# Attention output projection: two token tiles multiplied during the last attention units, and its input requested one group earlier

## The chip, the cores and the metric

The kernel runs on one core of a Trainium2 chip. The metric is the device time of one execution in microseconds (us). Engines are named as the profile names them: PE (TensorE, matrix products; PEld its weight loads), DVE (VectorE), ACT (ScalarE), POOL (GpSimd), SP (SyncE; SPq is its queue, from which this kernel issues all its DMAs).

## What is computed

For each of two images of 48 x 48 = 2304 tokens with 768 channels, in float32, one attention layer and one spectral layer, each added to its input:

```
q, k, v = split(groupnorm(x) @ qkv_w + qkv_b)              # 12 heads of 64
attn = softmax(q * 64**-0.5 @ k.T + rel_h + rel_w)         # rel_h, rel_w: products of q with tables
x = x + (attn @ v) @ proj_w + proj_b
f = rfft2(groupnorm(x))                                    # over the 48 x 48 grid
o1 = gelu(block_matmul(f, w1) + b1)                        # 8 blocks of 96 channels, complex
o2 = softshrink(block_matmul(o1, w2) + b2, 0.01)
x = x + irfft2(o2)
```

The change touches the line with proj_w, and the end of the attention ahead of it.

## The kernel before

The kernel is written in a tile framework. It derives the semaphores, and it chooses each engine's order of instructions when it builds the program: by program position among the instructions that it reckons ready. Instructions that go through the wrapper InOrder (L58) keep their program order on their engine; all of these carry L66 in the profile. The others can move.

The two images are handled one after the other (block_kernel, L1006), each in three stages.

*Attention* (L139). The unit of work is a pair of heads with 128 queries; there are 108 units (L451), numbered n. In the loop (L471) step n computes the scores of unit n (PE into PSUM banks, DVE adds the position term that POOL wrote into s, L320), the exponentials (ACT), and 32x32 transposes on DVE. exchange (L379) spreads them over the partitions into a buffer pT, of which there are two: per half unit six DMAs on SP and two ACT copies. weigh (L393) multiplies pT by the values two steps later: at step n it takes unit n-2. finish copies the result, and for every third unit writes it to the DRAM tensor oT; the inverses of the softmax denominators go to inv_d through a transpose ps_i. At the steps from 102 to 108 the loop calls late() (L533), which runs the next of seven steps of a Projection (L549): weights in two halves, nothing, tokens(0), nothing, the bias, and values_bias (L581). values_bias multiplies the value bias through the projection (L591), for the first image only. Its seventh call, at step 108, comes after weigh of unit 106 and ahead of weigh of unit 107 in the program.

tokens(g) (L602) fetches the attention output of 384 tokens (three token tiles of 128): one DMA from oT (L610), two from inv_d (L612), then one POOL multiply of the two (L616). There are two buffers for the product, taken in turn, and one for the inverses.

*Projection* (project_out, L620). x2 is six parts of x, each of four rows of 96 tokens. Each part is loaded (L632) and gets the projection bias on POOL, row by row (L634, four instructions a part). After part 0 come constants and tokens(1). Then the loop over 18 token tiles (L661): every third tile calls tokens for its group, if it isn't there yet, and takes it. For each half of the 768 output channels, six products (L670) go into one PSUM bank, and DVE adds the bank onto the rows of x2 (L679). Each float32 product is two matmul records in the profile, so a tile has 24. Between the tiles stand over_w (L642: eight matmul records ps_y, four ACT copies and a DMA to y_d, L658) and tile_stats (L700) for the finished rows: DVE sums (L703) and scales them (L704), POOL subtracts the mean (L706), ACT squares, DVE sums again (L710).

*Spectral* (L742) follows.

PSUM has seven banks in one pool, ps_b, for scores, projections, products and transforms, and one bank for ps_o. The projection's weights, bias, products and inverses lie in one SBUF area (tag span) that held the normalized x in attention before. The parts x2 take SBUF that attention's pools give back at its end.

```python
            if len(order) - 6 <= n <= len(order):
                late()
...
        if t % 3 == 0:
            if t // 3 not in pr.o:
                pr.tokens(t // 3)
            o_sb = pr.o[t // 3]
```

Of the kernel before, what the change touches and what calls it, by code (L numbers as in the profile page):

```python
# [9 lines left out]
F32 = mybir.dt.float32  # L10
# [6 lines left out]
P = 128  # L17
# [6 lines left out]
NCC = C // P  # L24
NT = S // P
# [7 lines left out]
UQ = 384  # L33
# [24 lines left out]
class InOrder:  # L58


    def __init__(self, tc, engine):
        self.tc, self.engine = tc, engine
# [474 lines left out]
def shifts(t):  # L537


    size = {0: P, 32: 32, 64: 64, 96: 32}  # L540
    p = 0
    while p < P:
        hp, q = divmod(t * P + p, 2 * HW)
        n = min(P - p, 2 * HW - q, size[p], size[q])
        yield p, hp, q, n
        p += n


class Projection:  # L549


    def __init__(self, tc, k, a, oT, inv_d, span, ps_b, dram):
        self.nc = nc = tc.nc
        self.k, self.a, self.ps_b, self.dram = k, a, ps_b, dram
        self.oT_v = oT.rearrange("(cc p) s -> p cc s", p=P)
        self.inv_d = inv_d
        self.whole = span.tile([P, NCC * S], F32, tag="span", name="proj")
        self.w = self.whole[:, : NCC * C].rearrange("p (cc f) -> p cc f", f=C)
        self.pb = self.whole[:, NCC * C : (NCC + 1) * C]
        self.o = {}  # L560
        w_v = a["proj_w"].rearrange("(cc p) f -> p cc f", p=P)
        half = NCC // 2
        self.steps = [
            lambda: nc.sync.dma_start(out=self.w[:, :half], in_=w_v[:, :half]),
            lambda: nc.sync.dma_start(out=self.w[:, half:], in_=w_v[:, half:]),
            lambda: None,
            lambda: self.tokens(0),
            lambda: None,
            self.bias,
            self.values_bias,  # L570
        ]

    def step(self):
        self.steps.pop(0)()
# [6 lines left out]
    def values_bias(self):  # L581


        nc, k = self.nc, self.k
        if k.pb_d is not None:
            return
        for hf in range(2):
            cols = slice(hf * UQ, (hf + 1) * UQ)
            ps = self.ps_b.tile([P, 512], F32, tag="b", name="ps_pb")
            for cc in range(NCC):  # L590
                nc.tensor.matmul(  # L591
                    ps[:, :UQ],
                    lhsT=k.bv[:, cc : cc + 1].to_broadcast([P, P]),
                    rhs=self.w[:, cc, cols],
                    start=(cc == 0),
                    stop=(cc == NCC - 1),
                )
            nc.vector.tensor_tensor(self.pb[:, cols], ps[:, :UQ], self.pb[:, cols], ALU.add)
        k.pb_d = self.dram.tile([C], F32, tag="pb_d", name="pb_d")
        nc.sync.dma_start(out=k.pb_d, in_=self.pb[0, :])  # L600

    def tokens(self, g):  # L602

        nc = self.nc
        at = [(NCC + 1) * C + i * NCC * UQ for i in range(3)]
        o_sb, inv = (
            self.whole[:, c0 : c0 + NCC * UQ].rearrange("p (cc s) -> p cc s", s=UQ)
            for c0 in (at[g % 2], at[2])
        )
        nc.sync.dma_start(out=o_sb, in_=self.oT_v[:, :, g * UQ : (g + 1) * UQ])  # L610
        for h in range(2):
            nc.sync.dma_start(  # L612
                out=inv[h * HD : (h + 1) * HD],
                in_=self.inv_d[:, g // 3, h, g % 3, :].partition_broadcast(HD),
            )
        nc.gpsimd.tensor_tensor(o_sb, o_sb, inv, ALU.mult)  # L616
        self.o[g] = o_sb


def project_out(tc, k, x_b, pr, pools, y_d, x2, stats, constants):  # L620

    nc = tc.nc
    ps_b, small, work = pools
    bank = lambda name: ps_b.tile([P, 512], F32, tag="b", name=name)
    R = 2 * HW
    x_v = x_b.rearrange("(t p) c -> p t c", p=R)  # L630
    for i, part in enumerate(x2):
        nc.sync.dma_start(out=part, in_=x_v[:, i * XP : (i + 1) * XP, :])  # L632
        for j in range(XP):
            nc.gpsimd.tensor_tensor(part[:, j, :], part[:, j, :], pr.pb[:R], ALU.add)  # L634
        if i == 0:
            constants()
            pr.tokens(1)
    row = lambda hp: x2[hp // XP][:, hp % XP, :]
    local = small.tile([R, HW // 2, NG], F32, tag="local", name="local")
    dev = small.tile([R, HW // 2, NG], F32, tag="dev", name="dev")  # L640

    def over_w(g):  # L642

        y1 = work.tile([YP, 2, C], F32, tag="y1", name="y1")
        part = x2[2 * g // XP]
        t0 = 2 * g % XP
        for s in range(C // SC):
            ch = slice(s * SC, (s + 1) * SC)
            ps = bank("ps_y")
            nc.tensor.matmul(  # L650
                ps[:YP, : 2 * SC],
                lhsT=k.fw,
                rhs=part[:, t0 : t0 + 2, ch],
                start=True,
                stop=True,
            )
            nc.scalar.copy(y1[:, :, ch], ps[:YP, : 2 * SC].rearrange("p (t c) -> p t c", c=SC))
        nc.sync.dma_start(out=y_d[:, 2 * g : 2 * g + 2, :], in_=y1)  # L658

    done = turned = 0  # L660
    for t in range(NT):  # L661
        if t % 3 == 0:
            if t // 3 not in pr.o:
                pr.tokens(t // 3)
            o_sb = pr.o[t // 3]
        for hf in range(2):
            cols = slice(hf * UQ, (hf + 1) * UQ)
            acc = bank("acc")
            for cc in range(NCC):
                nc.tensor.matmul(  # L670
                    acc[:, :UQ],
                    lhsT=o_sb[:, cc, (t % 3) * P : (t % 3 + 1) * P],
                    rhs=pr.w[:, cc, cols],
                    start=(cc == 0),
                    stop=(cc == NCC - 1),
                )
            for p, hp, q, n in shifts(t):
                dst = row(hp)[q : q + n, cols]
                nc.vector.tensor_tensor(dst, acc[p : p + n, :UQ], dst, ALU.add)  # L679
        while (turned + 1) * 2 * R <= (t - 1) * P:  # L680
            over_w(turned)
            turned += 1
        while (done + 1) * R <= (t + 1) * P:
            tile_stats(
                nc,
                lambda name: work.tile([R, C], F32, tag="st", name=name),
                row(done),
                local[:, done, :],
                dev[:, done, :],
            )  # L690
            done += 1
    while turned < HW // 4:
        over_w(turned)
        turned += 1
    mean, rstd = join_stats(nc, k, small, bank, local, dev)
    nc.vector.tensor_copy(stats[:, 0, :], mean)
    nc.vector.tensor_copy(stats[:, 1, :], rstd)


def tile_stats(nc, work, xt, local, dev):  # L700

    x3 = xt.rearrange("p (g d) -> p g d", d=GC)
    nc.vector.tensor_reduce(local, x3, AX.X, ALU.add)  # L703
    nc.vector.tensor_scalar(local, local, 1.0 / GC, None, ALU.mult)  # L704
    xc = work("st_xc").rearrange("p (g d) -> p g d", d=GC)
    nc.gpsimd.tensor_tensor(  # L706
        xc, x3, local[:, :, None].to_broadcast([xt.shape[0], NG, GC]), ALU.subtract
    )
    nc.scalar.activation(xc, xc, AF.Square)  # L709
    nc.vector.tensor_reduce(dev, xc, AX.X, ALU.add)  # L710
# [31 lines left out]
class Spectral:  # L742
# [50 lines left out]
    def bank(self, name):  # L793
        return self.ps_b.tile([P, 512], F32, tag="b", name=name)
# [363 lines left out]
```

## Time and profile before

| what | value |
|---|---|
| median of 3 runs | 3907.91 us (3903.24 to 3908.79) |
| the profiled execution | 3910.83 us |
| its span, first to last instruction | 3908.90 us |
| mean granted clock of PE | 0.967 |
| PE busy | 3660.4 us, 94% |
| DVE busy | 2987.5 us, 76% |
| ACT busy | 2528.1 us, 65% |
| POOL busy | 2117.0 us, 54% |
| products L670 | 864 records, 291.6 us busy, PE idle 24.5 us before them |
| POOL multiply L616 | 12 instructions, 5065 ns each |

The profile is one execution. Its times count from the span's start. A line of the view in order of time gives the start, the length, the engine, the line and the operation, what is written and read, the shape and how many instructions were merged; in brackets stands how long the engine was idle before and which work ended that. The chain of waits lists the start, the length and the piece of work. The first image's projection lies at about 1504 to 1694 us, the second's at about 3457 to 3647 us.

### The profile page before, as it was taken

What the parts mean: (1) busy time and instruction counts of PE and PEld (TensorE: products, weight loads), DVE (VectorE), ACT (ScalarE), POOL (GpSimd) and SP (SyncE); (2) the same over time, 40 slices, a digit from 0 to 9 for tenths busy, and PEclk for the clock granted to TensorE, in tenths of its full rate; (3) what the DMA queues carried; (4) which work ended last, traced back from release to release, by engine and by line L of the source; (5) the groups of instructions that cost most, each with busy time, mean ns of one, the idle gap of its engine ahead of it and who ended that gap; (6) DMA issues with size and microseconds to landing.
All of it is one profiled execution on the core that took longest, in us unless ns stands there. A gap on an engine that the chain in (4) does not pass through costs nothing.

```text
span 3908.9 us, 83210 instructions
## 1 busy us (share of the span) xinstructions
PE 3660.4 (94%) x31416; PEld 2591.6 (66%) x31416; DVE 2987.5 (76%) x6642; ACT 2528.1 (65%) x3585; POOL 2117.0 (54%) x682
## 2 busy tenths in 40 slices
PE   6999999999999888989959999999999999779898
PEld 4677776767777655566536777767677776545665
DVE  5688888888889885654546888888888888856544
ACT  3588888888888882222135888888888888722221
POOL 2566666666666666422225666666666666664221
PEclk7999999999999998999989999999999999989999
DMA  2477777777777888534424777777777778884344
GB/s 93 100 169 172 171 175 165 170 172 174 173 167 166 175 197 197 130 84 122 139 85 104 176 171 170 168 174 168 172 172 167 176 164 177 189 197 127 85 121 131
DMA packets 496094, 606.22 MB, mean 155 GB/s; under 512 B 180109, under 2 KB 311053, under 8 KB 495694
## 3 DMA queue, kind: packets, MB, share of 16 engines
q1 hardware_dynamic: 495694, 600.89, 66.1%
q8 instruction: 250, 4.10, 0.5%
q14 instruction: 150, 1.23, 0.1%
HBM read 130.81 MB, written 87.67 MB: 56 GB/s over the span
## 4 chain that ended last, share of the span: by engine, by line
PE 80%; DVE 6%; DMA 6%; POOL 4%; SPq 3%; issue 1%; ACT 1%; POOLq 0%; DVEq 0%; ACTq 0%
PE ps_o L66 20%; PE ps_s L66 19%; PE ps_proj L66 14%; PE ps_v L66 8%; PE acc L670 5%; DVE s L66 4%; PE ps L905 4%; POOL s L320 2%; SPq L66 2%; DMA pT<-s 2%; PE ps_z L853 2%; PE ps L878 2%; PE ps L882 2%; PE ps_u L936 2%; PE ps_r L66 1%
## 5 line engine op out<-in xcount | busy, mean ns | idle before, releaser
L320 POOL TENSOR_TENSOR s<-rhw 128x2304 f32<-128x2304 f32 x432 | 1744.8, 4060 | 1096.4 <-DMA pT<-s 575.9
L66 DVE CUSTOM_DVE_ANT_0 s<-ps_s,s 128x512 f32<-128x512 f32 (+1 forms) x2160 | 1223.3, 633 | 401.0 <-issue 225.6
L66 ACT ACTIVATE s<-s,nm 128x1152 f32<-128x1152 f32 x864 | 1074.7, 1245 | 445.9 <-DVE nm L66 415.1
L66 DVE STREAM_TRANSPOSE s<-s 128x1152 f32<-128x1152 f32 x864 | 1111.8, 1344 | 5.5 <-ACT s L66 5.5
L66 ACT COPY pT<-s 32x1152 f32<-32x1152 f32 x864 | 993.2, 1149 | 28.8 <-PE ps_o L66 13.3
L66 PE MATMUL ps_o<-pT,v 128*64 128x128 f32 x15552 | 924.5, 279 | 77.7 <-DMA pT<-s 41.7
L66 PEld LDWEIGHTS ps_o<-pT,v 128*64 128x64 f32 x15552 | 872.7, 140 | 140.6 <-issue 79.0
L66 PE MATMUL ps_s<-kT,qT 64*128 64x512 f32 (+1 forms) x4320 | 922.4, 559 | 23.2 <-DVE mx L66 19.3
L66 PEld LDWEIGHTS ps_s<-kT,qT 64*128 64x128 f32 x4320 | 432.5, 187 | 462.6 <-issue 335.6
L66 PE MATMUL ps_proj<-xnT,w 128*128 128x384 f32 (+1 forms) x2016 | 597.4, 450 | 11.8 <-issue 11.8
L66 PEld LDWEIGHTS ps_proj<-xnT,w 128*128 128x128 f32 x2016 | 360.5, 191 | 219.2 <-DVE mx L66 41.1
L670 PE MATMUL acc<-proj 128*128 128x384 f32 x864 | 291.6, 497 | 24.5 <-POOL proj L616 12.4
L66 PEld LDWEIGHTS ps_v<-w,xnT 128*128 128x128 f32 x2592 | 297.6, 194 | 21.8 <-DVE mx L66 21.8
L66 PE MATMUL ps_v<-w,xnT 128*128 128x128 f32 x2592 | 309.8, 279 | 0.0
L922 POOL TENSOR_TENSOR spectrum<-spectrum 128x480 f32<-128x480 f32 x80 | 96.2, 1203 | 326.7 <-DVE spectrum L921 323.9
L670 PEld LDWEIGHTS acc<-proj 128*128 128x128 f32 x864 | 168.0, 195 | 144.6 <-issue 21.3
L709 ACT ACTIVATE st_xc<-st_xc 96x768 f32<-96x768 f32 (+1 forms) x84 | 71.1, 847 | 266.7 <-POOL st_xc L706 266.7
L679 DVE TENSOR_TENSOR x<-acc,x 32x384 f32<-32x384 f32 (+2 forms) x216 | 119.5, 553 | 80.2 <-PE acc L670 76.3
L66 DVE DVE_READ_ACCUMULATOR2_ANT mx<- 128x1 f32 x2160 | 180.1, 83 | 0.0
L66 ACT ACTIVATION_READ_ACCUMULATOR s<-s,nm 128x1 f32 x864 | 161.2, 187 | 0.0
L710 DVE TENSOR_REDUCE dev<-st_xc 96x32 f32<-96x768 f32 (+1 forms) x84 | 78.9, 948 | 96.4 <-ACT st_xc L709 96.4
L706 POOL TENSOR_TENSOR st_xc<-x,local 96x768 f32<-96x768 f32 x48 | 70.9, 1481 | 148.2 <-DVE local L704 128.8
(87 smaller groups left out, 2275.1 us busy)
## 6 DMA issues: line engine op xcount, KB each, us to landing
pT<-s SPq DMA_DIRECT2D x2592, 144.0 KB
t<-rel SPq DMA_DIRECT2D x144, 189.0 KB
rhw<-t SPq DMA_DIRECT2D x144, 144.0 KB
y_d<-y SPq DMA_DIRECT2D x24, 672.0 KB
y<-y_d SPq DMA_DIRECT2D x40, 360.0 KB
u_d<-spectrum SPq DMA_DIRECT2D x40, 360.0 KB
u<-u_d SPq DMA_DIRECT2D x48, 300.0 KB
xt<-in_x SPq DMA_DIRECT2D x12, 1152.0 KB
```

What stands on the lines that cost most here:

```text
L66: return lambda *args, **kw: self.tc.keep_in_program_order(op(*args, **kw))
L320: nc.gpsimd.tensor_tensor(s[:, h, :].rearrange("p (y x) -> p y x", x=HW), rhw[:, x, h, :HW][:, :, None].to_broadcast([P, HW, HW]), rhw[:, ...
L670: nc.tensor.matmul(acc[:, :UQ], lhsT=o_sb[:, cc, (t % 3) * P : (t % 3 + 1) * P], rhs=pr.w[:, cc, cols], start=(cc == 0), stop=(cc == NCC - 1),
L679: nc.vector.tensor_tensor(dst, acc[p : p + n, :UQ], dst, ALU.add)
L709: nc.scalar.activation(xc, xc, AF.Square)
L710: nc.vector.tensor_reduce(dev, xc, AX.X, ALU.add)
L853: nc.tensor.matmul(ps[:BS, w * 96 : (w + 1) * 96], lhsT=self.y2[s, j][:, w, i * BS : (i + 1) * BS], rhs=k.fh, start=True, stop=True,)
L878: nc.tensor.matmul(ps[:BS, :400], lhsT=w1[:, wa, i, :], rhs=zf[:, 0, fs], start=True, stop=False,)
L882: nc.tensor.matmul(ps[:BS, :400], lhsT=w1[:, wb, i, :], rhs=zf[:, 1, fs], start=False, stop=True,)
L905: nc.tensor.matmul(ps[64 * r : 64 * r + 64, w * BS : (w + 1) * BS], lhsT=self.o1[:, ri, f0 : f0 + 64], rhs=w2[:, (0, 2, 1, 0)[2 * r + ri], ...
L922: nc.gpsimd.tensor_tensor(val, val, clip, ALU.subtract)
L936: nc.tensor.matmul(ps[: 2 * HW, :480], lhsT=k.ih, rhs=d2[:, c0 : c0 + 480], start=True, stop=True)
```

## The change

The seventh late step, still at step 108, is a new method last: values_bias as before, then the products of token tiles 0 and 1, in both halves, into four banks of ps_b that are kept in a dictionary accs. The projection loop takes these banks instead of computing them; DVE's adds stay where they were. Secondly, the loop asks for a group of tokens three tiles before it is used: at tile 3 for tiles 6 to 8, at tile 6 for tiles 9 to 11, and so on. Groups 0 and 1 are asked for where they were. The number of instructions doesn't change.

```diff
-            self.values_bias,
+            self.last,
         ]
+        self.accs = {}
...
+    def last(self):
+
+        self.values_bias()
+        for t in range(2):
+            for hf in range(2):
+                self.product(t, hf)
+
+    def product(self, t, hf):
+
+        o_sb = self.o[t // 3]
+        acc = self.ps_b.tile([P, 512], F32, tag="b", name="acc")
+        for cc in range(NCC):
+            self.nc.tensor.matmul(
+                acc[:, :UQ],
+                lhsT=o_sb[:, cc, (t % 3) * P : (t % 3 + 1) * P],
+                rhs=self.w[:, cc, hf * UQ : (hf + 1) * UQ],
+                start=(cc == 0),
+                stop=(cc == NCC - 1),
+            )
+        self.accs[t, hf] = acc
+
...
     for t in range(NT):
-        if t % 3 == 0:
-            if t // 3 not in pr.o:
-                pr.tokens(t // 3)
-            o_sb = pr.o[t // 3]
+        if t % 3 == 0 and 0 < t < NT - 3:
+            pr.tokens(t // 3 + 1)
         for hf in range(2):
             cols = slice(hf * UQ, (hf + 1) * UQ)
-            acc = bank("acc")
-            for cc in range(NCC):
-                nc.tensor.matmul(
-                    acc[:, :UQ],
-                    lhsT=o_sb[:, cc, (t % 3) * P : (t % 3 + 1) * P],
-                    rhs=pr.w[:, cc, cols],
-                    start=(cc == 0),
-                    stop=(cc == NCC - 1),
-                )
+            if (t, hf) not in pr.accs:
+                pr.product(t, hf)
+            acc = pr.accs.pop((t, hf))
```

## The prediction

> **What bounds the kernel now.** First the whole. TensorE (PE) is busy 94% of the span, but an early product helps only if PE is what comes last where its time is freed. Granted clock of the run: 0.967. So I read PE's instructions in order of time around the end of attention, then the same stretch on GpSimd (POOL) and on SyncE's queue (SPq). First batch, PE: unit 107's scores, then the attention weighting of units 105, 106 and 107 (ps_o), then the projection (L670).
>
> ```profile
> 1464.24 5.34 PE L66 MATMUL ps_s<-kT,qT 64*128 64x512 f32 x20
> 1469.51 8.01 PE L591 MATMUL ps_pb<-proj,bv 128*128 128x384 f32 x24
> 1478.88 4.15 PE L66 MATMUL ps_o<-pT,v 128*64 128x128 f32 x72 [1.37 <-DMA pT<-s]
> 1487.12 6.87 PE L66 MATMUL ps_o<-pT,v 128*64 128x128 f32 x72 [4.08 <-DMA pT<-s]
> 1497.13 6.98 PE L66 MATMUL ps_o<-pT,v 128*64 128x128 f32 x72 [3.14 <-DMA pT<-s]
> ...
> 1504.15 31.13 PE L670 MATMUL acc<-proj 128*128 128x384 f32 x96
> ...
> 1560.74 5.92 PE L670 MATMUL acc<-proj 128*128 128x384 f32 x12 [8.69 <-DVE x L679]
> 1572.63 7.78 PE L670 MATMUL acc<-proj 128*128 128x384 f32 x15 [5.96 <-POOL proj L616]
> ```
>
> The reader is to see two things. The weighting waits each time for the exchange (pT<-s), so there are holes of some 8.6 us that products could fill. And the projection is stopped later, before token tile 6: the 5.96 us wait ends with POOL's multiply of attention output by inverse denominators (L616) for tiles 6 to 8. From 1573 to 1694 the table of stretches shows PE busy 121.00 of 121 us. So the stage ends when tile 6 starts, plus a fixed PE-bound rest. **The start of tile 6 is the gate**; PE time saved before it is only waited away. So what does POOL do before it?
>
> ```profile
> 1516.03 5.06 POOL L616 TENSOR_TENSOR proj<-proj 128x2304 f32<-128x2304 f32 x1
> 1522.75 1.48 POOL L706 TENSOR_TENSOR st_xc<-x,local 96x768 f32<-96x768 f32 x1 [1.66 <-DVE local L704]
> 1524.20 14.17 POOL L634 TENSOR_TENSOR x<-x,proj 96x768 f32<-96x768 f32 x8
> 1538.33 2.92 POOL L706 TENSOR_TENSOR st_xc<-x,local 96x768 f32<-96x768 f32 x2
> 1541.21 14.15 POOL L634 TENSOR_TENSOR x<-x,proj 96x768 f32<-96x768 f32 x8
> 1555.54 1.48 POOL L706 TENSOR_TENSOR st_xc<-x,local 96x768 f32<-96x768 f32 x1 [0.18 <-DVE local L704]
> ...
> 1567.53 5.04 POOL L616 TENSOR_TENSOR proj<-proj 128x2304 f32<-128x2304 f32 x1 [1.79 <-DMA proj<-inv_d]
> ```
>
> POOL is full from 1522.75 to 1565.7: twenty bias adds on x (L634, 1.77 us each) and the statistics' subtractions (L706). Only then comes the gate's multiply, and it idles a mere 1.79 us for its data. SPq shows why the data is late:
>
> ```profile
> 1508.74 7.63 SPq L632 DMA_DIRECT2D x<-in_x  x5
> 1543.64 0.33 SPq L658 DMA_DIRECT2D y_d<-y  x1
> 1544.08 0.40 SPq L610 DMA_DIRECT2D proj<-oT  x1
> 1544.58 1.79 SPq L612 DMA_DIRECT2D proj<-inv_d  x1
> ...
> 1559.78 0.58 SPq L612 DMA_DIRECT2D proj<-inv_d  x1
> ```
>
> The request for tiles 6 to 8 stands behind a store (L658), its last half 15 us later. The second batch repeats it, 1953.15 us later: tile 6 starts at 3525.89. Its chain of waits has one more link that matters:
>
> ```profile
> 3431.82 5.64 PE ps_o L66 x72
> 3437.52 0.59 SPq L66
> ...
> 3445.24 5.41 DMA pT<-s
> 3450.96 6.30 PE ps_o L66 x72
> ```
>
> Weighting 105 releases the pT buffer into which unit 107 is exchanged: from its end to weighting 107 there are 13.5 us of DMA issue and landing (in the first batch from SPq's 1484.36 to 1497.13, 12.8 us). Work put ahead of weighting 105 therefore delays the end of attention one for one.
>
> [...] the 96x32 tensor_scalar of L704 needs 0.18 us when POOL is idle and 10.22 us at 1545.17, until the block of eight L634 ends. [...] the same 72 matmuls take 4.15 us behind work and 6.87 us after 4.08 us of idleness. [...] between 1510 and 1540 the DMA share is 1.00 to 1.07 at 223 to 233 GB/s[...].
>
> **The change, part by part.** I write d for the delay of attention's end.
>
> *Four products moved ahead.* A tile is 24 matmul records, 7.74 us in the chain (x24), so 0.3225 us each. Two tiles are 48 records, 15.5 us. They issue no DMA; they hold four of the seven PSUM banks, beside two of the bias product and one for the transpose ps_i, which fits. Their input is ready when L616 has run for tiles 0 to 2: 1476.27+5.10 = 1481.4 (second batch 3427.57+5.10 = 3432.7). Weightings 105 to 107 keep their order; products stand before weighting 107 in the program, so all are issued before it. What is unknown is how many, k, are issued before weighting 105, whose operands come at 1478.9 and 3431.8, about when the products' do. I take k near 0: weighting 105 is earlier in the program and its data come no later. The other end, k = 48, is a rival below.
>
> With k = 0, first batch: 1483.0 (end of 105) + 15.5 + 4.15 (106, warm) = 1502.7, weighting 107 ends at 1506.8 instead of 1504.1: d = 2.7. Second batch: 3437.4+15.5+4.15 = 3457.1, end 3461.2 instead of 3457.25: d = 4.0. Behind that end wait SPq's stores of oT and inv_d, the inverse loads for tiles 3 to 5 and x parts 1 to 5; all come d later. In exchange PE enters the stage with two tiles done, 15.5-d ahead, and has tiles 2 to 5 done around 1506.8+31+5.2 = 1543. This lead buys nothing at the gate.
>
> *What it buys on VectorE and POOL.* The adds of tile 0 no longer wait for PE (1508.28 now); they start with the first biased x rows, about 1503.5. The statistics of rows 0 and 1 come about as much sooner. POOL's idle time in front of the x block (5.70+1.66 us) then shrinks until the next limit: the inverse for tiles 3 to 5 lands at 1515+d, its multiply ends at 1520+d, and the twenty bias adds start there, not at 1524.2. First batch: 1522.7, a gain of 1.5. Second batch: L616 started at 3469.43 on its data, so 3469.43+5.06+4.0 = 3478.5, against 3477.34: a loss of 1.2.
>
> *Request three tiles ahead.* Nothing is added: three DMAs (L610, L612 twice) and one multiply a group, moved from tile 6 to tile 3, and so on. On SPq they go behind the five x parts and ahead of the y_d store, waiting there only for tile 2's products and the L616 before; behind them wait the y_d stores, which PE then doesn't need soon. Their 2.36 MB at 228 GB/s take 10.4 us after the x parts (landed at 1540.2): 1551+d, against 1567.4. So the 1.79 us (second batch 1.89) of waiting on POOL go. But the multiply stays behind the bias adds, which are earlier in the program and whose data land earlier; what is late next is POOL itself. With the same four subtractions (rows 2 to 5) before it as now, the gate moves by 1.5+1.8 = 3.3 us and by -1.2+1.9 = 0.7 us, 4.0 together. If rows 6 and 7 also get ahead of it, 1.48 x 2 = 3.0 a batch are lost; if rows 4 and 5 fall behind it, 3.0 a batch are won. PE stands idle longer before tile 6: the first 24 records take 10.3 to 10.7 us there now; a colder start (ps_z at 3658.46: 8.29 for 50 records instead of 4.25) may cost up to 1 more a batch; I take 0.5.
>
> Later groups: tile 9's multiply ended at 1586.4 while PE needed it about 1601, so asking earlier gains nothing. Hidden by POOL's 43 us block: all of the product lead. If that cover went, up to 15.5-d a batch would show.
>
> **Sum.** 4.0-1.0 = 3.0 us off the profiled execution's 3910.83 (span 3908.90 and 1.93 around it). That execution is 2.9 over the median 3907.91. Against the median: **3905**.
>
> **Rivals.** *The queues come out better (B).* If the multiply for tiles 6 to 8 goes right behind the last bias add, it ends at 1522.7+35.4+5.05 = 1563.2 (gain 9.4) and 3478.5+40.5 = 3519.0 (gain 6.9): 16 together, **3892**; ahead of the last four adds another 7.1 a batch, 3878. For it: its data are there by 1554, and VectorE's statistics may be too late for POOL. Against: the bias adds come first in the program, and subtractions fit while x is loading.
>
> *Slower (C): products ahead of weighting 105.* The bias product of the first batch (L591) already stands there, pulled ahead of weightings 105 and 106, which speaks for it; the late L616 speaks against. With k = 48 weighting 105 starts at 1481.4+15.5 = 1496.9, ends at 1501.0, and 12.8 us later weighting 107 starts at 1513.8 instead of 1497.13: d = 16.7. Second batch 3432.7+15.5+4.15+13.5 = 3465.9 instead of 3450.96: d = 15. The x parts go with it: 4.2-16.7+1.8 = -10.7 and 2.8-15+1.9 = -10.3, **3929**. It decides from the point where 107's exchange ends later than PE: 1481.4+0.3225k+4.15+12.8 over 1505.1, k over 21; at k = 34 it is about half.
>
> *The products aren't moved in effect:* if PE's order leaves them behind weighting 107, d = 0 and only the earlier request counts, some 4 us: inside the forecast's case.
>
> **Chances.** Forecast, 3900 to 3911: 0.41. B, 3878 to 3899: 0.36. C, over 3916: 0.23. A measurement of this kernel can tell about 0.2%, 7.8 us, from no change, so the forecast counts as the same, B as faster, C as slower. Range 3885 to 3925: it leaves out the upper half of C and the best end of B.
>
> **What would show it.** PE: four acc products between weightings 105 and 107, no holes there, 107 ending 3 to 4 us later; then 15 us or more of idleness before tile 6, ended by L616. POOL: no wait for inv_d before that multiply, the bias adds still ahead of it. SPq: L610 right behind the x parts. I am wrong if the multiply for tiles 6 to 8 stands before the last bias adds, if weighting 105 comes after the products, or if VectorE, not POOL, ends the wait before tile 6.

## The result and the profile after

| | before | after |
|---|---|---|
| median of 6 runs | 3906.57 us (3903.24 to 3908.79) | 3924.93 us (3921.81 to 3926.38) |
| the profiled execution, its span | 3910.83 us, 3908.90 us | 3924.16 us, 3922.40 us |
| mean granted clock of PE | 0.967 | 0.966 |
| PE idle before the products | 24.5 us | 64.9 us |
| busy time of the products | 291.6 us | 298.9 us |

The ratio is 1.0047, with a 95% interval of 1.0034 to 1.0060: the change costs 18.4 us. That is near rival C's 3929, not the forecast's 3905. The two profiled executions stand 13.3 us apart.

First PE in order of time, from unit 107's scores on, as in the prediction, first image. L615 is the line of the products now.

```profile
1469.81 8.01 PE L592 MATMUL ps_pb<-proj,bv 128*128 128x384 f32 x24
1481.33 10.99 PE L615 MATMUL acc<-proj 128*128 128x384 f32 x28 [3.51 <-POOL proj L638]
1492.25 4.15 PE L66 MATMUL ps_o<-pT,v 128*64 128x128 f32 x72
1496.33 6.72 PE L615 MATMUL acc<-proj 128*128 128x384 f32 x20
1502.98 4.15 PE L66 MATMUL ps_o<-pT,v 128*64 128x128 f32 x72
1510.70 6.92 PE L66 MATMUL ps_o<-pT,v 128*64 128x128 f32 x72 [3.57 <-DMA pT<-s]
...
1517.67 7.91 PE L615 MATMUL acc<-proj 128*128 128x384 f32 x24
1534.95 10.65 PE L615 MATMUL acc<-proj 128*128 128x384 f32 x24 [9.37 <-POOL proj L638]
...
1581.66 9.49 PE L615 MATMUL acc<-proj 128*128 128x384 f32 x24 [15.41 <-POOL proj L638]
```

The three lines with ps_o are weightings 105, 106 and 107. 28 of the 48 new records stand ahead of weighting 105, and PE waits 3.51 us for POOL's product of tiles 0 to 2 before it can begin them. Weighting 105 starts at 1492.25, where it started at 1478.88. The products fill the holes, but weighting 107 ends 13 us later. After it PE, two tiles ahead, stands still before token tiles 3 and 6 (9.37 and 15.41 us), both times for POOL. The second image, the same view:

```profile
3438.98 10.30 PE L615 MATMUL acc<-proj 128*128 128x384 f32 x22 [9.04 <-POOL proj L638]
3449.22 4.15 PE L66 MATMUL ps_o<-pT,v 128*64 128x128 f32 x72
3453.30 8.65 PE L615 MATMUL acc<-proj 128*128 128x384 f32 x26
3461.88 4.15 PE L66 MATMUL ps_o<-pT,v 128*64 128x128 f32 x72
3466.82 4.15 PE L66 MATMUL ps_o<-pT,v 128*64 128x128 f32 x72 [0.79 <-ACT res L66]
...
3490.80 10.64 PE L615 MATMUL acc<-proj 128*128 128x384 f32 x24 [11.87 <-POOL proj L638]
...
3537.75 11.06 PE L615 MATMUL acc<-proj 128*128 128x384 f32 x24 [15.66 <-POOL proj L638]
```

Here 22 records are ahead of weighting 105, and PE waits 9.04 us for the multiply before it can begin them. The chain of waits of the kernel after (start, length, piece) ties the first image together:

```profile
1476.19 5.09 POOL proj L638
1481.33 10.99 PE acc L615 x28
1492.32 4.11 PE ps_o L66 x72
...
1504.41 6.05 DMA pT<-s
...
1510.70 6.94 PE ps_o L66 x72
...
1524.05 27.02 DMA x<-in_x
...
1576.60 5.02 POOL proj L638
1581.66 9.49 PE acc L615 x24
```

The moved products are themselves on the path: POOL's multiply, 28 records, weighting 105, the exchange into the buffer that it released, weighting 107, the stores, the x parts (the load on the path in at 1551.07, 1536.88 before), the bias adds, the multiply for tiles 6 to 8, tile 6. The table of waits on SP's queue, from 1470 to 1520 (total, times, longest), shows the joint; before there is no such line in this stretch.

```profile
SPq L66 <- PE ps_o L66: 12.6, 1, 12.6
```

On POOL (in order of time) the stretch ahead of tile 6 has the order that the prediction gave it, only later:

```profile
1529.85 5.04 POOL L638 TENSOR_TENSOR proj<-proj 128x2304 f32<-128x2304 f32 x1
1535.52 2.92 POOL L720 TENSOR_TENSOR st_xc<-x,local 96x768 f32<-96x768 f32 x2 [0.63 <-DVE local L718]
1538.40 14.17 POOL L656 TENSOR_TENSOR x<-x,proj 96x768 f32<-96x768 f32 x8
1552.52 1.49 POOL L720 TENSOR_TENSOR st_xc<-x,local 96x768 f32<-96x768 f32 x1
1553.97 21.19 POOL L656 TENSOR_TENSOR x<-x,proj 96x768 f32<-96x768 f32 x12
1575.11 1.49 POOL L720 TENSOR_TENSOR st_xc<-x,local 96x768 f32<-96x768 f32 x1
1576.55 5.05 POOL L638 TENSOR_TENSOR proj<-proj 128x2304 f32<-128x2304 f32 x1
```

Twenty bias adds (L656) and four subtractions (L720), then the multiply (L638), now without a wait for its data. SP's queue asked for those data in time, right behind the x parts:

```profile
1522.22 7.41 SPq L654 DMA_DIRECT2D x<-in_x  x5
1529.67 5.53 SPq L632 DMA_DIRECT2D proj<-oT  x1
1535.30 14.15 SPq L634 DMA_DIRECT2D proj<-inv_d  x2
1549.55 9.81 SPq L680 DMA_DIRECT2D y_d<-y  x2
```

**Where the time went.** I count each image from the end of unit 107's scores, so that what came earlier drops out. In us, first image / second image; differences in the text are taken before rounding:

| kernel | weighting 107 ends | tile 6 starts | projection ends (last ps_y) |
|---|---|---|---|
| before | 34.5 / 32.6 | 103.0 / 101.2 | 224.7 / 222.4 |
| after | 47.7 / 41.0 | 111.8 / 107.8 | 232.2 / 229.8 |
| e1, products alone | 42.6 / 40.7 | 119.9 / 119.0 | 240.6 / 240.0 |
| e2, early request alone | 34.1 / 35.2 | 100.8 / 101.9 | 221.4 / 222.6 |
| e3, products behind weighting 106 | 42.0 / 42.0 | 109.4 / 109.3 | 229.9 / 231.2 |
| e4, the change, gate opened | 42.7 / 41.7 | 91.5 / 92.3 | 214.1 / 214.9 |
| e9, no products, gate opened | 33.9 / 33.9 | 85.5 / 85.5 | 212.5 / 211.4 |
| e10, the change, same gate as e9 | 47.5 / 40.9 | 96.0 / 91.3 | 217.4 / 214.9 |
| e11, one tile, same gate as e9 | 35.2 / 33.9 | 81.1 / 84.6 | 200.0 / 203.5 |

The balance of this stretch, after against before: delay of weighting 107, 13.2 / 8.5; PE's waits behind it, 9.37+15.41 against 8.69+5.96, so 10.1 more, and in the second image 11.87+15.66 against 6.4+3.4 on products and 3.4 on ps_y, so 14.3 more; work taken out, 15.5 an image. That is 13.2+10.1-15.5 = 7.8 and 8.5+14.3-15.5 = 7.3, where the table has 7.5 and 7.4. Both add to 15, beside 13.3 between the profiled executions and 18.4 (13.3 to 23.4 by the interval) between the medians. The rest of the program varies more than that: over the fourteen profiles the first image's scores end between 1469.6 and 1478.6, and the way from the first image's last ps_y to the second image's last score takes 1723.6 to 1733.2 us. So the times of single profiles are compared only inside this stretch.

### The profile page after: what moved, and what is told of

Read it like the earlier page. It is cut to its first block, busy times and chain, and to the rows that moved or that the text cites. A ratio compares the mean times of both kernels' runs of the same rounds, so it can differ in the third digit from the quotient of the medians.

```text
span 3922.4 us, 83199 instructions
## 1 busy us (share of the span) xinstructions
PE 3655.9 (93%) x31416; PEld 2587.5 (66%) x31416; DVE 2985.3 (76%) x6642; ACT 2529.2 (64%) x3585; POOL 2116.6 (54%) x682
## 4 chain that ended last, share of the span: by engine, by line
PE 82%; DMA 5%; DVE 5%; POOL 4%; SPq 2%; issue 2%; ACT 1%; POOLq 0%; DVEq 0%
PE ps_o L66 21%; PE ps_s L66 19%; PE ps_proj L66 14%; PE ps_v L66 8%; PE acc L615 6%; PE ps L919 4%; DVE s L66 2%; PE ps_z L867 2%; POOL s L320 2%; PE ps_u L950 2%; PE ps L892 2%; PE ps L896 2%; SPq L66 2%; DMA pT<-s 1%; PE ps_r L66 1%
## 5 line engine op out<-in xcount | busy, mean ns | idle before, releaser
L615 PE MATMUL acc<-proj 128*128 128x384 f32 x864 | 298.9, 506 | 64.9 <-POOL proj L638 64.9
L615 PEld LDWEIGHTS acc<-proj 128*128 128x128 f32 x864 | 170.6, 199 | 188.0 <-POOL proj L638 68.3
L720 POOL TENSOR_TENSOR st_xc<-x,local 96x768 f32<-96x768 f32 x48 | 70.9, 1481 | 144.9 <-DVE local L718 136.1
```

What stands on the lines that cost most here:

```text
L615: self.nc.tensor.matmul(acc[:, :UQ], lhsT=o_sb[:, cc, (t % 3) * P : (t % 3 + 1) * P], rhs=self.w[:, cc, hf * UQ : (hf + 1) * UQ], start=(c ...
```

## The experiments

Theories. **H**: the products delay weighting 107, and with it everything that waits for attention's end. **Q**: the early request costs the time, by crowding SP's queue or POOL. **K**: the early work (PSUM banks held by the products, DVE's adds) costs it. **G**: whatever starts earlier, POOL's block of bias adds holds the multiply for tile 6 (the gate), so a lead is lost there. Each run stood beside runs of the kernel before on the same chip.

**e1_products_only.** The products are moved, the request stays where it was.

```diff
-        if t % 3 == 0 and 0 < t < NT - 3:
-            pr.tokens(t // 3 + 1)
+        if t % 3 == 0 and t // 3 not in pr.o:
+            pr.tokens(t // 3)
```

> The products of tiles 0 and 1 moved as in the change, each group of tokens asked for only when its first tile comes, as before. Theory H (products in front of weighting 105 hold the pT buffer, the exchange of unit 107 and the end of attention come 13 to 14 us later in each image): this part alone brings the whole loss, +15 to +25 us against the kernel before, with weighting 107 again near 1510 to 1518. Rival Q (the early request is what costs: SP's queue held for 14 us, its transfer beside x and the inverses): no loss, -5 to +3 us.

Measured: 3948.55 against 3911.14, ratio 1.0093 (1.0079 to 1.0107), twice the loss of the change. So the loss comes with the products, and the early request doesn't cause it: it takes half of it away. POOL, first image, in order of time, shows how:

```profile
1552.75 21.18 POOL L656 TENSOR_TENSOR x<-x,proj 96x768 f32<-96x768 f32 x12
1574.14 1.48 POOL L720 TENSOR_TENSOR st_xc<-x,local 96x768 f32<-96x768 f32 x1 [0.21 <-DVE local L718]
1584.12 2.92 POOL L720 TENSOR_TENSOR st_xc<-x,local 96x768 f32<-96x768 f32 x2 [8.50 <-DVE local L718]
1587.01 5.04 POOL L638 TENSOR_TENSOR proj<-proj 128x2304 f32<-128x2304 f32 x1
```

With the multiply at its old place in the program, rows 6 and 7 are subtracted ahead of it, and for these POOL waits 8.50 us on DVE. PE stands 27.87 us before tile 6.

**e2_ahead_only.** The early request alone, in the kernel before.

```diff
-            if t // 3 not in pr.o:
-                pr.tokens(t // 3)
+            if 0 < t < NT - 3:
+                pr.tokens(t // 3 + 1)
```

> Only the request three tiles ahead; the products stay where they were. Theory H: POOL's queue still holds the multiply for tiles 6 to 8 behind the last bias add, so at best the 1.8 us a batch of waiting for its data go: -4 to +1 us against before. Rival Q: +13 to +20 us.

Measured: 3908.11 against 3911.14, 0.9993 (0.9985 to 1.0002), so a small gain or none. Theory Q falls. In front of the multiply for tiles 6 to 8 POOL no longer waits for data, PE's wait before tile 6 shrinks to 4.20 and 4.26 us, and no more: the bias adds still stand in front.

**e3_ordered.** The change, with the products queued on PE behind weighting 106, whose last matmul the late step finds in behind.

```diff
+                tc.behind = older["done"].ins
                 late()
...
         self.values_bias()
-        for t in range(2):
-            for hf in range(2):
-                self.product(t, hf)
+        with self.tc.issue_after(self.tc.behind):
+            for t in range(2):
+                for hf in range(2):
+                    self.product(t, hf)
```

> The change, with the four products queued behind weighting 106 on PE, so that none stands before weighting 105. Theory H: the end of attention is 3 to 5 us later than before instead of 13.5, and the start of tile 6 within 3 us of before: -5 to +5 us against before, so 14 to 22 us of the change's loss gone. A second rival K (the banks that the products hold, or the early adds, cost): as slow as the change, +15 to +20 us.

Measured: 3925.22 against 3911.14, 1.0038 (1.0025 to 1.0050): 14.1 us are lost with no product ahead of weighting 105. This refutes H in its narrow form, that the place ahead of weighting 105 alone is to blame, and comes close to what K forecast. PE, first image, in order of time:

```profile
1484.99 4.15 PE L66 MATMUL ps_o<-pT,v 128*64 128x128 f32 x72
1491.83 5.82 PE L66 MATMUL ps_o<-pT,v 128*64 128x128 f32 x72 [2.69 <-ACT res L66]
1497.58 15.75 PE L618 MATMUL acc<-proj 128*128 128x384 f32 x48
1513.25 4.15 PE L66 MATMUL ps_o<-pT,v 128*64 128x128 f32 x72
```

The hole between weightings 105 and 106 stays empty (2.69 us), and two tiles are longer than the hole behind 106: weighting 107 ends 7.4 and 9.4 us later than before, with PE itself the limit. Also the request for tiles 3 to 5 moved behind the stores on SP's queue (issued at 1521.46), and tile 3 waited 13.17 us for its multiply. How the loss divides between these two was not separated. For K nothing shows: from weighting 107 to the last ps_y the tables of PE's waits of this kernel name POOL's multiply alone, and no wait for a bank.

**e4_gate_after.** The change, with x parts 3 to 5 loaded and biased between the tiles instead of ahead of them, so that POOL's block before tile 6 has eight adds and not twenty. load_x loads a part on SP and adds its bias on POOL, both in program order.

```diff
-    for i, part in enumerate(x2):
+    for i in range(3):
...
+        if t in (4, 7, 10):
+            load_x(3 + (t - 4) // 3, sync, pool_q)
```

> The change as it is, products in front of weighting 105 included; only parts 3 to 5 of x are loaded and biased later (at tiles 4, 7 and 10), so that on POOL the multiply for tiles 6 to 8 comes after 8 instead of 20 bias adds. If POOL's queue is the gate for tile 6 (my prediction's step), that multiply comes some 15 to 20 us earlier, PE's lead of two tiles is used, and the time falls by 20 to 35 us against the change, below the kernel before: -5 to -18 us against before. If the x loads, the request's transfer or VectorE are the limit, less than 8 us against the change.

Measured: 3899.60 against 3911.14, 0.9972 (0.9961 to 0.9983). Tile 6 starts 20.3 and 15.5 us sooner than after, in both images without any wait of PE for it. POOL, first image, in order of time:

```profile
1540.29 14.16 POOL L659 TENSOR_TENSOR x<-x,proj 96x768 f32<-96x768 f32 x8
1554.42 1.48 POOL L728 TENSOR_TENSOR st_xc<-x,local 96x768 f32<-96x768 f32 x1
1555.86 5.07 POOL L638 TENSOR_TENSOR proj<-proj 128x2304 f32<-128x2304 f32 x1
```

The multiply for tiles 6 to 8 now runs right behind eight adds, at 1555.86 instead of 1576.55. This confirms G: the block of adds is the gate. The wait before tile 3 remains (10.60 us).

**e5_gate_ahead** is the same gate edit with the products where they were, **e6_gate_ordered** with two tiles behind weighting 106.

> Products as before the change; request three tiles ahead; parts 3 to 5 of x loaded and biased at tiles 4, 7 and 10. Theory G (POOL's block of 20 bias adds is the gate for tile 6, and products ahead only cost): PE is never stopped before tile 6, so the way from the last score to the end of the projection falls from 224.7 and 222.4 us by some 14 to 19 us an image, the time by 28 to 38 us against before; faster than the change with the same edit. Rival (the lead of two tiles is worth its delay once the gate is open): slower than that kernel, gain under 12 us.

> The products of two tiles queued behind weighting 106, and the gate opened as in the run before. Attention ends 7 to 9 us later as in the ordered kernel without it, and tile 3 waits some 10 us for its inverses; PE has two tiles (15.5 us) done. Theory G: no better than the kernel with products as before, gain 15 to 30 us against before. Rival (lead worth its price): gain over 38 us.

Measured: e5 3906.37 against 3911.45, 0.9988 (0.9981 to 0.9995); e6 3898.88, 0.9970 (0.9959 to 0.9982). Both gain less than was expected, and e6 more than e5, where G had it the other way. e5 should have gained more: tile 6 starts at 86.4 and 85.2 in the measure of the table, but the projection ends at 221.0 and 220.0. A late part of x is the cause. POOL of e5, then PE of e5, in order of time:

```profile
1592.45 7.10 POOL L66 TENSOR_TENSOR x<-x,proj 96x768 f32<-96x768 f32 x4 [10.80 <-DMA x<-in_x]
```

```profile
1605.26 1.59 PE L656 MATMUL ps_y<-x,fw 96*112 96x384 f32 x2 [6.10 <-DVE x L685]
```

The load of the part stood behind y_d stores, POOL waited for it, DVE for POOL, PE for DVE. So e5 is no clean base for e4 and e6, and e9 below mends it. In e6, as in e4, PE's waits for DVE there are 1.4 us at most; e8 below has the long wait again (5.74 and 6.0 us).

**e7_one_tile** is the change with tile 0 alone moved; **e8_gate_one_ordered** has one tile, behind weighting 106, and the gate edit of e4.

```diff
-        for t in range(2):
+        for t in range(1):
```

> The change with the products of tile 0 alone moved (24 records). On PE 24 of them (first image) and 22 (second) stand in front of weighting 105, as against 28 and 22 in the change. Theory H (what stands in front of weighting 105 delays the exchange of unit 107): the end of attention stays 9 to 12 and 8 to 9 us later than before, and the loss stays at two thirds or more of the change's, +8 to +18 us. Rival (the sum of all moved records counts, whatever their place): half, +4 to +9 us, with the end of attention 4 to 7 us later.

> One tile's products, queued behind weighting 106 and ahead of 107, where the exchange of unit 107 leaves PE about 9 us free: 24 records are 7.7 us and should fit, so the end of attention moves by 0 to 2 us only. With the gate open as in the two runs before: up to 7.7 us an image better than products as before, if tile 3's inverses and VectorE let it: gain 25 to 45 us against before. If the products still push attention's end by 4 us or more, the hole isn't there.

Measured: e7 3924.90 against 3911.45, 1.0033 (1.0020 to 1.0046); e8 3892.25, 0.9953 (0.9939 to 0.9966), less than the 25 us or more that were expected. Halving the products leaves most of the loss, because the half that stays is the one ahead of weighting 105. PE of e7:

```profile
1485.60 9.70 PE L615 MATMUL acc<-proj 128*128 128x384 f32 x24 [3.33 <-POOL proj L638]
1495.23 4.15 PE L66 MATMUL ps_o<-pT,v 128*64 128x128 f32 x72
```

All 24 records are ahead of weighting 105 (22 in the second image), and weighting 107 ends 9.4 and 11.3 us later than before. In e8 the same 24 fit the hole behind 106: the end of 107 moves by -0.4 and +1.1. The gate edit lies behind weighting 107, so for one tile this is the place alone. For two tiles the place made no difference that could be told: e3 against the change, e6 against e4.

**e9 to e12** share a second gate edit. x parts 3 to 5 are loaded right behind the early request at tile 3, and biased at tiles 4, 7 and 10.

```diff
+            if t == 3:
+                for i in range(3, 6):
+                    load_x(i)
...
+        if t in (4, 7, 10):
+            bias_x(3 + (t - 4) // 3, pool_q)
```

e9_gate2_ahead leaves the products where they were, e10_gate2_after is the change, e11_gate2_one has one tile behind weighting 106, and e12_gate2_one_early besides asks for tiles 3 to 5 in the last late step.

> As the kernel with products as before and the gate opened, but parts 3 to 5 of x are loaded right behind the early request instead of at tiles 4, 7 and 10 behind y_d stores; only their bias adds stay late. In that kernel tile 6 began 16 us earlier after the last score, and VectorE, waiting for the late bias adds, took it back at tiles 8 to 12. If that is where it went, the way from the last score to the end of the projection falls by 12 to 18 us an image instead of 3: 20 to 35 us faster than before. If VectorE's own chain takes it back, still under 8 us.

> The change with the same edit. If products in front of weighting 105 only cost (attention's end 8 to 13 us later, tile 3 waiting 10 us), it is no faster than the run before in this list: 10 to 30 us faster than the kernel before the change. If the lead of two tiles pays once nothing else holds tile 6, it is faster than that run by 5 us or more.

> One tile's products behind weighting 106, with the same edit: attention's end moves by 0 to 3 us, one tile (7.7 us) is done early. If the hole in front of weighting 107 is worth filling, 3 to 7 us an image better than products as before, so 30 to 45 us faster than the kernel before; if not, within 5 us of products as before.

> The same, and the second group (tiles 3 to 5) asked for in the last late step, so that its multiply runs in attention's tail and not behind the last stores; part 0 of x comes behind those stores in return. If tile 3's wait for its inverses is what the new gate is, it goes, and the time falls by another 4 to 12 us; if x part 0 then comes too late, the gain is lost again.

Measured against 3909.70: e9 3885.97, 0.9936 (0.9923 to 0.9948); e10 3894.56, 0.9956 (0.9943 to 0.9968); e11 3867.84, 0.9890 (0.9877 to 0.9904); e12 3874.38, 0.9901 (0.9886 to 0.9916). Two tiles partly ahead of weighting 105 cost 8.6 us against none; one tile in the hole gains 18.1 us over the two images, of which 2 x 7.9 are the tile's own time. The two kernels differ in the number of tiles as well as in their place. e12's early request took tile 3's wait away, but put x part 0 behind it (POOL waited 4.63 us for it), and gained nothing. PE of e11, first image:

```profile
1490.62 6.64 PE L66 MATMUL ps_o<-pT,v 128*64 128x128 f32 x72 [4.26 <-DMA pT<-s]
1497.19 8.01 PE L618 MATMUL acc<-proj 128*128 128x384 f32 x24
1505.13 4.15 PE L66 MATMUL ps_o<-pT,v 128*64 128x128 f32 x72
...
1526.74 8.01 PE L618 MATMUL acc<-proj 128*128 128x384 f32 x24 [1.77 <-POOL proj L641]
...
1547.49 15.64 PE L618 MATMUL acc<-proj 128*128 128x384 f32 x48
```

From weighting 107 to the last ps_y of this image the 1.77 us before tile 3 are the only wait that the table of waits names; before has 14.65 us there. Tiles 5 and 6 run in one piece at 1547.49. e11 is the fastest version found, 1.1% under the kernel before.

Not tried: a third pT buffer, which would take the exchange of unit 107 off weighting 105; and one tile ahead of weighting 105 with the gate open.

## Why the prediction was wrong

**The failed step is d, the delay of attention's end, and first the k in it.** The prediction had d = 2.7 and 4.0; measured are 13.2 and 8.5. It took k, the records ahead of weighting 105, "near 0: weighting 105 is earlier in the program and its data come no later". k was 28 and 22. The program position held, and so did the data: in before the operands of weighting 105 were in at 1478.88, and those of the products at 1481.4. But the framework fixes PE's order when it builds the program, from what it then reckons ready, and a trace shows only when things came in. The one line that bore on that choice was the bias product of the same late step, already ahead of 105 in before; the prediction named it, and gave it too little weight. In the second image there is no bias product, and 22 records went ahead all the same, 9.04 us of waiting included.

**What d became.** "One for one" was right in the first image: counted from unit 107's scores, weighting 105 came 13.1 us later, 107 13.2 us. Rival C's formula with k = 28 gives 10.2 (1481.4+9.0+4.15+12.8-1497.13). Two terms of it were too small. After 3.51 us of idleness, at a granted clock of 0.84, the 28 records took 10.99 us instead of 28 x 0.3225 = 9.0. And the 12.8 us count from an SPq instruction at 1484.36; from the end of weighting 105 (1483.03) it was 14.1 before and is 14.3 after. The other 20 records lie in time that the exchange takes anyway. In the second image PE, not the exchange, is last: 107 follows 106 after 0.79 us, d is 8.5.

**k is not the whole of it.** In e3, the nearest case to k = 0 that was built, d was too small as well: forecast 2.7 and 4.0, e3 7.4 and 9.4. First image, from the end of 105 to the end of 107: 15.5+4.15+4.15 = 23.8 by the prediction, 1517.4-1489.1 = 28.3 in e3. The difference is the hole of 2.69 that could not be filled (weighting 106 waits there for ACT's copy of the one ps_o bank) and 5.82-4.15 = 1.67 of a slower weighting, 4.4 in all. An order with k = 0 and products on both sides of weighting 106, as the prediction drew it, was not run; what it would have lost stays open.

**The wait before tile 3** was not in the prediction, though its own numbers held it: the multiply for tiles 3 to 5 was to end at 1520+d, that is at 1522.7, and PE, two tiles ahead, was to reach tile 3 near 1506.8+7.9 = 1514.7: some 8 us. It came to 9.37 and 11.87 us. With the gate closed PE stands longer before tile 6 in any case; with the gate open this wait is what is left (10.60 us in e4).

**The gate was right.** Tile 6 is started by POOL's multiply behind twenty bias adds and four subtractions, PE stood 15.41 and 15.66 us before it ("15 us or more"), and opening the block by e4's edit brings tile 6 forward by 20.3 and 15.5 us. That "the stage ends when tile 6 starts, plus a fixed PE-bound rest" held with the gate closed: 121.7 and 121.2 us before, 120.5 and 122.0 after. With the gate open the rest is not fixed: 118.9 in both images of e11, 127.0 and 125.9 in e9, 134.6 and 134.8 in e5. That the lead "buys nothing at the gate" fits the waits of after, but a lead with 107 undelayed and the gate closed was not run, so this stays open. With the gate open one tile is worth 18.1 us.

**The shift of the gate, by the prediction's own formula.** 4.2-d+1.8 with d = 13.2 gives -7.2, that is 7.2 later; measured 8.7 later. Second image 2.8-8.5+1.9 = -3.8, measured 6.6 later. So with the right d the formula explains 11.0 of 15.3. Of the first image's rest, the multiply of tiles 3 to 5 ended at 1534.89, 1.7 after the assumed 1520+d = 1533.2. So rival C was the right case, at a d between its k = 48 and none. That its 3929 lies only 4 us from the measured 3924.93 is in part luck: its d was 16.7 and 15, 10 us more in all than measured, and what the formula leaves out (4 us here) and the scatter of the rest of the program went the other way.

**The early request was right alone, and mis-sized beside the products.** By itself it was worth 3.0 us (between -0.8 and 5.9), near the forecast's 1.8+1.9, though it can't be told from nothing. "If rows 6 and 7 also get ahead of it, 1.48 x 2 = 3.0 a batch are lost" counted only POOL's own time. In e1, where they did, tile 6 starts 8.1 and 11.2 us later than in after, although weighting 107 ends 5.1 and 0.3 us sooner: POOL waits 8.50 us for DVE's scaling of those rows first. The subtractions in front of a queued multiply cost what they wait for, not what they last.

**The slower restart** (0.5 an image): the first 24 records of tile 6 took 9.49 and 11.06 us, at a granted clock of 0.84 and 0.72, against 10.68 and 10.27 us before, at 0.74 and 0.78. No cost that could be told.

**What stands of the theories.** H in its wider form: whatever puts work ahead of weighting 107 for longer than its hole lasts delays all that waits for attention's end, and with the old gate the work that it takes out is not won back. The runs with 107 late by 7 us or more and the old gate all lose (after, e1, e3, e7); e11 and e8, with 107 late by at most 1.4, gain most beside the kernels with the same gate edit. G stands as well. K has nothing for it: e11 holds two banks early and has DVE's adds early, and gains; four banks held early were not tested by themselves, but between weighting 107 and the last ps_y the tables of PE's waits of after name POOL's multiply alone, and no bank.

## What to carry to other kernels

Work that is moved into the holes of a chain must go behind the link that releases the next transfer, and must not be longer than the hole there. Ask of each hole how long it is and whose order decides that the work lands in it; where a framework chooses, the place is a thing to set, and not to infer from arrival times in a trace. One tile of 7.9 us in the right hole of each image was worth 18 us with the gate open; two tiles cost, partly ahead of the link (e10 against e9) or wholly in a hole too short for them (e3).

Before work is given a lead, look for the next gate on another engine. Here it was a block of adds that stood in front of a multiply in one queue; opening it was worth 24 us with no product moved (3 of them the early request's), and then one tile's lead paid.

## What the runs showed of the hardware

DVE's scaling of a 96x32 tile took 0.18 us at 1528.09 in after, with POOL idle. In the second image it took 14.99 us, to the end of POOL's run of twelve adds at 3531.0, and inside the like run of the first image 0.92 us. Behind the like run of e1, over at 1573.93, POOL waits another 0.21 us for such a scaling. In order of time on DVE, in after:

```profile
3516.06 14.99 DVE L718 TENSOR_SCALAR local<-local 96x32 f32<-96x32 f32 x1
```

```profile
1560.21 0.92 DVE L718 TENSOR_SCALAR local<-local 96x32 f32<-96x32 f32 x1
```

One add lasts 1.77 us. The scaling at 3516.06 lasted as long as some eight adds that stood back to back; the one at 1560.21 was over in 0.92 us, while POOL's adds went on to 1575.16. What decides between the two is not shown.

The same 72 matmuls took 4.15 us behind work and 5.82 us after 2.69 us of idleness in the first images of e3, e7 and e8. But in the second image of before a hole of the same length left them at 4.15 us and a granted clock of 1.00:

```profile
3440.12 4.15 PE L66 MATMUL ps_o<-pT,v 128*64 128x128 f32 x72 [2.68 <-ACT res L66]
```

Holes of 2.90 us in before went both ways as well: 4.15 us at a granted clock of 1.00 (at 1275.92), 5.82 us at 0.71 (1348.35), 6.98 us at 0.58 (3261.81). So a hole of 2.7 to 2.9 us was followed by slower matmuls in some places and not in others; what decides is not shown.
